# A four-layer graph network on one core: the recurrent part of n in seven block products, and the input part accumulated onto r times it

## The chip, the cores and the metric

The kernel runs on one core of a Trainium2 chip. The metric is the device time of one execution in microseconds. Three runs of the kernel before took 3054.23, 3055.60 and 3055.82 us; their median, 3055.6 us, is the time before. The engines are named as in the profile: PE is TensorE (PEld its weight loads), DVE is VectorE, ACT is ScalarE, POOL is GpSimd, SP is SyncE, which issues most of the DMAs.

## The reference

The input is 64 graphs of 256 nodes with 256 features, and one adjacency matrix (0 or 1) for each. Four layers follow one another, each of the form `x = x + layer(relu(layernorm(x)), adj)`. Layers 0, 1 and 2 are graph attention layers (four heads, four heads with a layer norm, one head). Layer 3 is a gated graph network: three rounds of aggregation over the adjacency and a GRU cell. The change touches the GRU cell alone:

```python
def _gru_cell(inp, h, w_ih, w_hh, b_ih, b_hh):
    gi = inp @ w_ih.T + b_ih
    gh = h @ w_hh.T + b_hh
    i_r, i_z, i_n = jnp.split(gi, 3, axis=-1)
    h_r, h_z, h_n = jnp.split(gh, 3, axis=-1)
    r = jax.nn.sigmoid(i_r + h_r)
    z = jax.nn.sigmoid(i_z + h_z)
    n = jnp.tanh(i_n + r * h_n)
    return (1.0 - z) * n + z * h
...
for i in range(L):
    m = jnp.einsum('bnd,de->bne', h, weight[i])
    aggr = jnp.einsum('bst,bsd->btd', A, m)
    h = _gru_cell(aggr, h, w_ih, w_hh, b_ih, b_hh)
```

Everything is fp32. `h_n` is called the recurrent part of n in what follows, and `i_n` its input part.

## The kernel before, in words

**Units.** `_fast_path` works through 33 units: one graph alone, then 31 pairs of graphs, then one graph alone (`units`). `graphs(u, first, nb)` lists the work of a unit of nb graphs: `layer0`, `layer1`, `layer2`, `gru`. A pair has S = 512 columns (nodes of graph 0, then of graph 1), N = 256 for each graph. Features lie on the 128 partitions in two chunks, `dc` for the features that are summed over and `j` for those that come out.

**Order of the work.** Nothing is issued while the work is listed. `op()` records each operation with its engine, an assumed cost, and the buffers it reads and writes, and `_Schedule` plans all of it at once. `paths()` gives first due times from the end of each unit (a multiple of `PACE`) back along the dependences, each step priced at `STRETCH` times the cost plus `MARGIN`. `play()` then goes forward in time: an idle engine takes the operation that is due first among those whose predecessors are done and whose buffers have a free slot. A result reaches another engine `HOP` ns after the operation ends. `latest()` plays the same work backwards for the next round's due times; after seven rounds at most the shortest plan is kept. The outcome is a fixed instruction order on each engine, so several units are in flight at once, and an engine that waits holds up all that is behind it. `HOP`, `STRETCH`, `MARGIN`, `PACE` and the costs given to `op()` take part in this plan alone; they issue nothing.

**Buffers.** The planner hands out fixed numbers of slots (lines 893 to 903), among them 13 of class `g` (128x512 fp32 partial results), 8 PSUM banks, 2 `ht3_` (the state h, transposed), 2 `ag` (the aggregated messages), 1 `am_r` (the adjacency), 3 `sw` (weight sums fetched from DRAM), 1 `turn`.

**The GRU of a pair, one round.** `aggregate` makes `ag` from `h` and the adjacency. The message weights have been multiplied into the input weights during setup (`wc`), so `ag` stands for the aggregated h. Then:

- `hidden(j, ...)`, for j = 0 and 1: `gate` multiplies `whh`'s block for n with the state `ht`, two matmuls of 512 columns into a bank of its own, and ScalarE moves the sum to SBUF with half the recurrent bias (`n`).
- `products` computes the sums for r and z. The four blocks (r or z, graph 0 or 1, state and message together) are arranged so that seven products of 256x256 by 256x256 serve where eight would: differences `t1` to `t4` on VectorE, seven calls of `product` (four matmuls of 256 columns each), and `kept` (ScalarE copies a bank to SBUF) or `added` (VectorE adds a bank to a buffer) after them. Three banks are used: `ps_s`, `ps_t`, `ps_w`.
- `unit(j, ...)`: ScalarE takes tanh of r (the sigmoids are written by tanh of half the argument); VectorE multiplies r with `n`; `gate` puts the input part into a new bank `ps_i`, two matmuls of 512 columns; VectorE adds it to `n` from PSUM; ScalarE takes tanh; z follows, and three VectorE operations make the new state, in place.
- `rows_of` transposes the new state for the next aggregation, or for the output.

Units of one graph go through `plain`, which the change leaves alone. In the profile, `gate`'s matmuls are L1477, `product`'s L1575, `aggregate`'s L1463, the differences in `products` L1567, and all that is recorded by `vec` is L912, whatever it is.

## Time and profile before

| what | value |
|---|---|
| median of three runs | 3055.6 us (3054.23 to 3055.82) |
| the profiled execution's own time | 3056.75 us |
| its span, first to last instruction | 3054.7 us |
| mean granted TensorE clock | 0.993 |
| busy: PE, PEld, DVE, ACT, POOL | 98%, 78%, 83%, 69%, 14% of the span |
| DMA | 212.43 MB, mean 70 GB/s |
| chain that ended last | PE 95% (L1575 37%, L1477 23%, L1267 12%, L1158 11%), DVE 2%, ACT 1%, DMA 1% |

All durations in the profile come from one profiled execution; its time is 1.15 us over the median of the runs, and its span 2.05 us under its own time. A line of a group reads: source line, engine, operation, output<-inputs, shapes, count, then busy time in us and mean ns of one, then the idle time of the engine ahead of these instructions and what ended it. A TensorE matmul of fp32 appears as two records, with a weight load ahead of each. Ends of matmuls are modelled, and their durations overlap; the time from one start to the next is the pace. A line of waits reads: who waited, for whom, us in total, how often, the longest.

### The profile page before, as it was taken

The page shows a single profiled execution, that of the slowest core. Times are in us where ns is not written, and L with a number is a line of the kernel's source. Part 1 is how long each engine was busy: PE and PEld are TensorE (multiplying, and loading weights), DVE is VectorE, ACT ScalarE, POOL GpSimd, SP SyncE. Part 2 cuts the span into 40 slices and gives each one's busy share as a digit, 9 for nine tenths or more (in the row PEclk, how much of TensorE's full clock was granted, in tenths as well). Part 3 has the DMA queues.
Part 4 walks back from the last instruction along what each step waited for, and adds up shares of the span by engine and source line. Part 5 has one row for each costly group of instructions (what it writes and reads, how often), then busy time and mean ns, then how long its engine had stood idle before and what let it go on. Part 6 is the DMA issues. An engine that isn't in the chain of part 4 may idle for free.

```text
span 3054.7 us, 56348 instructions
## 1 busy us (share of the span) xinstructions
PE 3000.5 (98%) x20900; PEld 2370.9 (78%) x20900; DVE 2533.0 (83%) x5933; ACT 2109.2 (69%) x4811; POOL 430.3 (14%) x643
## 2 busy tenths in 40 slices
PE   8799999999999999999999999999999999999998
PEld 7677787777787777787777787777777777787777
DVE  7876878888988888988888988888988888988764
ACT  7676667767776767766767766767776766766554
POOL 3311101111111111111111111111111111101100
PEclk9899999999999999999999999999999999999999
DMA  4111222221222122222121222221222221121110
GB/s 139 59 50 47 69 67 90 61 81 59 81 81 77 60 80 60 80 81 76 61 80 58 82 81 73 63 81 56 84 80 70 66 81 57 60 79 56 45 49 24
DMA packets 150936, 212.43 MB, mean 70 GB/s; under 512 B 49239, under 2 KB 102013, under 8 KB 143229
## 3 DMA queue, kind: packets, MB, share of 16 engines
q1 hardware_dynamic: 146752, 207.40, 21.7%
q8 instruction: 167, 2.74, 0.4%
q10 hardware_dynamic: 3900, 1.34, 0.2%
q14 instruction: 117, 0.95, 0.1%
HBM read 180.62 MB, written 19.68 MB: 66 GB/s over the span
## 4 chain that ended last, share of the span: by engine, by line
PE 95%; DVE 2%; ACT 1%; DMA 1%; issue 0%; POOL 0%; SPq 0%; ACTq 0%; DVEq 0%
PE bank L1575 37%; PE bank L1477 23%; PE bank L1267 12%; PE bank L1158 11%; PE bank L1463 6%; PE bank L1136 4%; PE bank L1491 3%; PE bank L1195 1%; DVE pt L912 1%; DVE g L912 0%; DVE o L912 0%; PE bank L1211 0%; PE bank L1032 0%; ACT g L912 0%; DMA xt<-in_x_dram 0%
## 5 line engine op out<-in xcount | busy, mean ns | idle before, releaser
L912 ACT ACTIVATE g<-g,bg 128x256 f32<-128x256 f32 (+1 forms) x756 | 393.9, 555 | 164.4 <-DVE g L912 96.6
L912 DVE SCALAR_TENSOR_TENSOR pt<-pt,f,cap 128x256 f32<-128x256 f32 x1152 | 476.2, 479 | 11.9 <-ACT pt L1248 10.1
L1248 ACT ACTIVATE pt<-cb,f 128x256 f32<-128x256 f32 x1062 | 441.3, 504 | 4.2 <-PE bank L1267 3.7
L1267 PEld LDWEIGHTS bank<-wh,pt 128*64 128x64 f32 (+1 forms) x8704 | 345.5, 141 | 85.5 <-issue 62.3
L1267 PE MATMUL bank<-wh,pt 128*64 128x65 f32 (+1 forms) x8704 | 391.3, 233 | 6.5 <-DVE pt L912 2.7
L912 DVE TENSOR_TENSOR g<-bank,g 128x512 f32<-128x512 f32 x279 | 191.4, 686 | 241.6 <-PE bank L1575 234.3
L1477 PE MATMUL bank<-ht,whh 128*128 128x512 f32 (+1 forms) x888 | 379.4, 561 | 0.0
L1477 PE MATMUL bank<-ag,wc 128*128 128x512 f32 (+1 forms) x888 | 377.9, 558 | 0.1
L1575 PE MATMUL bank<-g,sw 128*128 128x256 f32 x1488 | 349.8, 381 | 2.7 <-DVE g L1567 2.7
L912 DVE SCALAR_TENSOR_TENSOR g<-g,g 128x512 f32<-128x512 f32 (+1 forms) x396 | 257.2, 670 | 80.7 <-ACT g L912 80.5
L1575 PEld LDWEIGHTS bank<-g,sw 128*128 128x128 f32 x1488 | 278.7, 190 | 44.9 <-issue 4.5
L912 ACT ACTIVATE g<-bank,bg 128x256 f32<-128x256 f32 (+1 forms) x408 | 224.6, 568 | 108.3 <-PE bank L1477 97.6
L912 ACT COPY g<-bank 128x512 f32<-128x512 f32 x279 | 162.6, 583 | 187.8 <-PE bank L1575 181.9
L1477 PEld LDWEIGHTS bank<-ag,wc 128*128 128x128 f32 x888 | 164.4, 190 | 129.1 <-issue 120.1
L1477 PEld LDWEIGHTS bank<-ht,whh 128*128 128x128 f32 x888 | 161.1, 190 | 122.3 <-issue 103.6
L1463 PE MATMUL bank<-am_r,hl 128*128 128x256 f32 x1536 | 233.7, 301 | 0.0
L1119 ACT ACTIVATE xn<-xt,mv 128x256 f32<-128x256 f32 x384 | 210.5, 597 | 24.6 <-DVE mv L912 22.9
L1463 PEld LDWEIGHTS bank<-am_r,hl 128*128 128x128 f32 x1536 | 196.2, 189 | 31.8 <-issue 21.7
L1101 DVE BATCH_NORM_STATS2 st<-xt 128x6 f32<-128x256 f32 x512 | 207.9, 406 | 10.1 <-DMA xt<-in_x_dram 9.9
L912 ACT COPY ht<-bank 128x512 f32<-128x512 f32 (+1 forms) x264 | 143.4, 575 | 101.5 <-PE bank L1136 101.3
L1110 POOL TENSOR_SCALAR mv<-mv 128x4 f32<-128x4 f32 (+1 forms) x132 | 48.3, 366 | 1152.1 <-DVE mv L1102 1029.6
L1575 PE MATMUL bank<-ht,whh 128*128 128x256 f32 x744 | 180.2, 386 | 0.4 <-ACT ht L912 0.4
(113 smaller groups left out, 5389.9 us busy)
## 6 DMA issues: line engine op xcount, KB each, us to landing
sw<-sd SPq DMA_DIRECT2D x279, 256.0 KB, 2.7
cb<-rd SPq DMA_DIRECT2D x58, 1024.0 KB, 4.7
xt<-in_x_dram SPq DMA_DIRECT2D x31, 512.0 KB, 4.0
at<-in_adj_dram SPq DMA_DIRECT2D x31, 512.0 KB, 3.8
out_dram<-xt SPq DMA_DIRECT2D x31, 512.0 KB, 2.9
cb<-rd SPq DMA_DIRECT2D x29, 256.0 KB, 3.3
sd<-g SPq DMA_DIRECT2D x9, 256.0 KB, 2.3
cap<-cap_n SPq DMA_TRANSPOSE x128, 2.3
```

The source lines that it names most:

```text
L912: emit = lambda: fn(*[a() if callable(a) else a for a in args], **kw)
L1101: nc.vector.bn_stats(st.tile[:, c, :], xt.tile[:, c, :])
L1110: nc.gpsimd.tensor_scalar(mv.tile[:, 2, :], mv.tile[:, 1, :], 1e-5, None, op0=OP.add)
L1119: op("act", 610, lambda: nc.scalar.activation(xn.tile[:, c, :], xt.tile[:, c, :], AF.Relu, bias=mv.tile[:, 3, c : c + 1], scale=mv.tile[:, ...
L1136: nc.tensor.transpose(ps.tile[:, c * P : (c + 1) * P], xn.tile[:, c, dc * P : (dc + 1) * P], ident)
L1158: nc.tensor.matmul(ps.tile[:, : heads * W], lhsT=ht.tile[:, dc, c * P : (c + 1) * P], rhs=we[:, dc].rearrange("p h w -> p (h w)"), start=( ...
L1248: op("act", 500, lambda: nc.scalar.activation(pt.tile[:, b, jc, :], source(h, b), AF.Exp, scale=slope - 1.0, bias=f.tile[:, 1, h, c : c + ...
L1267: nc.tensor.matmul(ps[q * Q : (q + 1) * Q], lhsT=pt.tile[:, b, jc, i0 : i0 + Q], rhs=wh.tile[:, h, 2 * b + jc, :w], start=(jc == 0), stop= ...
L1463: nc.tensor.matmul(ps.tile[:, b * N : (b + 1) * N], lhsT=hl.tile[:, k, 2 * b + sc, :], rhs=am.tile[:, 2 * b + sc, :], start=(k == 0 and sc ...
L1477: nc.tensor.matmul(ps.tile[:, :S], lhsT=w[:, dc, g * P : (g + 1) * P], rhs=v.tile[:, dc, :], start=(first and dc == 0), stop=(last and dc ...
L1491: nc.tensor.transpose(ps.tile[:, c * P : (c + 1) * P], ht.tile[:, j, c * P : (c + 1) * P], ident)
L1575: nc.tensor.matmul(ps.tile[:, j * N : (j + 1) * N], lhsT=w()[:, dc, j * P : (j + 1) * P], rhs=view()[:, dc], start=(first and j == 0 and d ...
```

## The change

For pairs of graphs, `hidden` is rewritten. The four blocks of the recurrent part of n (output block j = 0 or 1, graph 0 or 1), each a sum over two chunks dc, are now computed with seven products of a 128x128 weight block by 128x256 columns in place of eight: four sums and differences of `whh`'s blocks for n are made once in setup (`sh`), three differences of state blocks for each round (`t23` with two parts, `t4`, beside `t1`, which is shared with `products`), and the products go to two banks, from which four ScalarE moves (`kept`) and three VectorE additions (`added`) build `ns`. A product that adds onto a half bank comes after the move that reads that half.

`unit` no longer takes a bank for the input part. VectorE writes (r+1) times `n` into a bank that `products` has finished with (`ps_w` for j = 0, `ps_t` for j = 1), the two `gate` matmuls accumulate the input part onto it, and ScalarE takes tanh straight from PSUM with the scale in the same instruction. The VectorE addition of the input part is gone. The recurrent part is now kept at scale 0.5 in all rounds, which needs a second copy of the bias (`bg` has ten columns).

The planner's constants change too: `PACE`, `HOP`, `STRETCH`, `MARGIN`, and the cost assumed for `aggregate`.

```diff
-PACE = 93600
+PACE = 93800
...
-    HOP = {"pe": 370, "act": 240, "dve": 240, "pool": 270, "sp": 0}
+    HOP = {"pe": 340, "act": 210, "dve": 210, "pool": 240, "sp": 0}
...
-    STRETCH = 3.79
-    MARGIN = 500
+    STRETCH = 3.43
+    MARGIN = 1100
...
+    block_of = lambda j, dc: whh[:, dc, 2 * D + j * P : 2 * D + (j + 1) * P]
+    less(lambda: sh[:, 0], lambda: block_of(1, 0), lambda: block_of(1, 1), [B_whh], [(B_sh, 0)], OP.add, 280)
+    less(lambda: sh[:, 1], lambda: sh[:, 0], lambda: block_of(0, 0), [B_whh, (B_sh, 0)], [(B_sh, 1)], cost=280)
+    less(lambda: sh[:, 2], lambda: block_of(0, 0), lambda: block_of(1, 0), [B_whh], [(B_sh, 2)], cost=280)
+    less(lambda: sh[:, 3], lambda: block_of(0, 1), lambda: sh[:, 1], [B_whh, (B_sh, 1)], [(B_sh, 3)], cost=280)
...
+        nc.vector.tensor_copy(bg[:, 8:10], bh.tile[:, 4:6])
...
-                op("pe", pe(1060), emit, [hl, am], [ps], takes=[ag])
+                op("pe", pe(1125), emit, [hl, am], [ps], takes=[ag])
...
-            def gate(ps, w, B_w, g, v, first, last):
+            def gate(ps, w, B_w, g, v, first, last, onto=False):
...
+                            skip_group_check=onto,
...
-                def hidden(j, ht, half):
-                    n, ps_h = g_tile(), bank()
-                    gate(ps_h, whh, B_whh, 4 + j, ht, True, True)
-                    vec(nc.scalar.activation, act(700), lambda: n.tile, lambda: ps_h.tile[:, :S], AF.Identity,
-                        bias=bg[:, 4 + j : 5 + j], scale=half, reads=[ps_h, B_bg], writes=[n], engine="act")
-                    return n
+                def hidden(ht, t1):
+
+                    ns = [g_tile() for _ in range(DC)]
+                    t23, t4 = buf("g", [P, 2, N]), buf("g", [P, N])
+                    ps_s, ps_w = bank(), bank()
+                    of = lambda g, dc: ht.tile[:, dc, g * N : (g + 1) * N]
+                    lo, hi = slice(0, N), slice(N, S)
+                    b0 = 4 if i == 0 else 8
+
+                    def less_of(out, x_, y_, reads, writes):
+                        op("dve", 415, lambda: nc.vector.tensor_tensor(out(), x_(), y_(), op=OP.subtract), reads, writes, port=True)
+
+                    def product(ps, where, w, v, reads, first=False):
+                        op("pe", 432, lambda: nc.tensor.matmul(
+                            ps.tile[:, where], lhsT=w, rhs=v(), start=first, stop=False, skip_group_check=True,
+                        ), [*reads, B_whh, B_sh], [ps])
+
+                    def kept(j, out, ps, where):
+                        vec(nc.scalar.activation, 440, lambda: ns[j].tile[:, out], lambda: ps.tile[:, where], AF.Identity,
+                            bias=bg[:, b0 + j : b0 + j + 1], scale=0.5, reads=[ps, B_bg],
+                            writes=[(ns[j], out.start)], engine="act")
+
+                    def added(j, out, ps, where):
+                        vec(nc.vector.scalar_tensor_tensor, 450, lambda: ns[j].tile[:, out], lambda: ps.tile[:, where], 0.5,
+                            lambda: ns[j].tile[:, out], op0=OP.mult, op1=OP.add, reads=[ps], writes=[(ns[j], out.start)])
+
+                    less_of(lambda: t23.tile[:, 1], lambda: of(1, 1), lambda: of(1, 0), [ht], [(t23, 1)])
+                    less_of(lambda: t23.tile[:, 0], lambda: of(1, 1), lambda: t1.tile[:, 0], [ht, t1], [(t23, 0)])
+                    less_of(lambda: t4.tile, lambda: of(0, 1), lambda: t23.tile[:, 0], [ht, (t23, 0)], [t4])
+                    product(ps_s, lo, block_of(0, 0), lambda: of(0, 0), [ht], True)
+                    product(ps_s, hi, block_of(0, 1), lambda: of(0, 1), [ht])
+                    kept(0, lo, ps_s, lo)
+                    added(0, lo, ps_s, hi)
+                    product(ps_w, lo, sh[:, 2], lambda: t23.tile[:, 1], [(t23, 1)], True)
+                    kept(1, hi, ps_w, lo)
+                    product(ps_s, lo, sh[:, 1], lambda: t23.tile[:, 0], [(t23, 0)])
+                    kept(1, lo, ps_s, lo)
+                    product(ps_s, lo, sh[:, 0], lambda: t1.tile[:, 0], [t1])
+                    added(1, hi, ps_s, lo)
+                    product(ps_w, lo, block_of(1, 1), lambda: t4.tile, [t4])
+                    added(1, lo, ps_w, lo)
+                    product(ps_s, lo, sh[:, 3], lambda: of(1, 1), [ht])
+                    kept(0, hi, ps_s, lo)
+                    return ns
...
-                    return (t2, t3), p1, ps_s
+                    return (t2, t3), p1, ps_s, (ps_w, ps_t)
...
-                    d, ps_i = g_tile(), bank()
+                    d, ps_n = g_tile(), free[j]
...
-                    vec(stt, dve(700), lambda: n.tile, lambda: d.tile, 1.0, lambda: n.tile,
-                        op0=OP.add, op1=OP.mult, reads=both, writes=[n], port=True)
-                    gate(ps_i, wi, B_wc, 4 + j, ag, True, True)
-                    vec(stt, dve(720), lambda: n.tile, lambda: ps_i.tile[:, :S], 2 * half, lambda: n.tile,
-                        op0=OP.mult, op1=OP.add, reads=[ps_i], writes=[n])
-                    vec(nc.scalar.activation, act(730), lambda: n.tile, lambda: n.tile, AF.Tanh,
-                        bias=bg[:, 6 + j : 7 + j], reads=[B_bg], writes=[n], engine="act")
+                    vec(stt, dve(700), lambda: ps_n.tile[:, :S], lambda: d.tile, 1.0, lambda: n.tile,
+                        op0=OP.add, op1=OP.mult, reads=[n, *both], writes=[ps_n], port=True)
+                    gate(ps_n, wi, B_wc, 4 + j, ag, False, True, True)
+                    vec(nc.scalar.activation, act(700), lambda: n.tile, lambda: ps_n.tile[:, :S], AF.Tanh,
+                        bias=bg[:, 6 + j : 7 + j], scale=2 * half, reads=[ps_n, B_bg], writes=[n], engine="act")
...
-                    ns = [hidden(j, ht, half) for j in range(DC)]
-                    rz = products(i, ht, ag, wi)
+                    t1 = buf("g", [P, DC, N])
+                    vec(nc.vector.tensor_tensor, 700, lambda t1=t1: t1.tile, lambda ht=ht: ht.tile[:, :, N:],
+                        lambda ht=ht: ht.tile[:, :, :N], op=OP.subtract, reads=[ht], writes=[t1], port=True)
+                    ns = hidden(ht, t1)
+                    rz = products(i, ht, t1, ag, wi)
```

## The prediction

> **What bounds the kernel now.** I read first the page's engine totals, then TensorE's waits, then the groups by shape, then the order in time, then the windows. The totals:
>
> ```profile
> span 3054.7 us, 56348 instructions
> PE 3000.5 (98%) x20900; PEld 2370.9 (78%) x20900; DVE 2533.0 (83%) x5933; ACT 2109.2 (69%) x4811; POOL 430.3 (14%) x643
> ```
>
> TensorE is 98% busy, but modelled matmul ends can hide gaps, so the view that decides is who TensorE waited for:
>
> ```profile
> PE bank L1136 <- ACT xn L1119: 29.0, 2, 14.8
> PE bank L1491 <- DVE ht L912: 3.9, 3, 1.9
> PE bank L1491 <- DVE hl L912: 2.8, 1, 2.8
> ```
>
> Two waits of 14.8 and 14.2 us, both before 105 us, are most of it. The same view cut to 400 to 2800 us is empty: there TensorE waits for nobody. So time is TensorE's instruction count times its pace. The pace comes from start-to-start times (columns: start, us, engine, line, op, count):
>
> ```profile
> 1570.61 3.60 PE L1477 MATMUL bank<-ag,wc 128*128 128x512 f32 x8
> 1574.04 1.89 PE L1575 MATMUL bank<-ag,wc 128*128 128x256 f32 x8
> 1575.77 0.60 PE L1136 MATMUL bank<-ident,xn 128*128 128x128 f32 x4
> ```
>
> Eight 512-column records take 1574.04-1570.61 = 3.43 us, 429 ns each; eight 256-column ones 1.73 us, 216 ns each. The mean durations (596 and 381 ns in the groups) are latencies that overlap and must not be summed. Each fp32 matmul is two records: 31 pairs of graphs x 3 GRU layers x 2 blocks j x 2 chunks dc = 372 matmuls is 744 records, as this group says:
>
> ```profile
> L1477 PE MATMUL bank<-ht,whh 128*128 128x512 f32 x744 | 344.5, 596 | 0.0
> L1575 PE MATMUL bank<-g,sw 128*128 128x256 f32 x1488 | 349.8, 381 | 2.7 <-DVE g L1567 2.7
> ```
>
> Who comes next? The steady pattern repeats every pair (chain pieces at 626.58, 718.39, 810.17 us: about 92 us). One period, and its two parts (columns: stretch, length, then busy us of PE, PEld, DVE, ACT, POOL):
>
> ```profile
> 1510.00:1581.00 71.00, 71.00 (x545) 54.00 (x544) 67.79 (x164) 49.87 (x111) 10.67 (x13) 1.00 0.21 63
> 1581.00:1592.00 11.00, 11.00 (x52) 9.63 (x51) 2.29 (x6) 7.19 (x16) 2.42 (x6) 1.00 0.12 30
> 1500.00:1592.00 92.00, 92.00 (x646) 72.44 (x645) 78.58 (x182) 65.97 (x150) 13.20 (x19) 1.00 0.23 73
> ```
>
> VectorE has 78.6 of 92 us, 85%, but unevenly: 95% for 71 us, then nearly idle for 11. It is the next limit.
>
> [...] a load takes 190 ns, yet 256-column records with a new load each start every 216 ns. [...]
>
> **The change part by part.** Per pair and GRU layer:
>
> *TensorE.* Removed: hidden()'s 4 matmuls of 512 columns, 8 x 429 = 3432 ns. Added: 7 of 256, 14 x 216 = 3024 ns. Saved 408 ns; x 93 = 37.9 us. The input gates keep their 4 matmuls; only their place moves. No other TensorE work changes.
>
> *Weight loads.* Six more records per layer: 6 x 190 ns x 93 = 106 us of load time, to some 2477 us (82%). Costed at nothing: each hides under a 216 ns matmul, with 26 ns to spare. Without that cover the price would be at most those 106 us.
>
> *VectorE.* The rows:
>
> ```profile
> L912 DVE SCALAR_TENSOR_TENSOR g<-bank,g 128x512 f32<-128x512 f32 x186 | 124.3, 684 | 14.0 <-PE bank L1477 13.8
> L912 DVE SCALAR_TENSOR_TENSOR g<-bank,g 128x256 f32<-128x256 f32 x12 | 5.1, 424 | 5.1 <-PE bank L1477 5.0
> L912 DVE TENSOR_TENSOR o<-o,beta_b 128x256 f32<-128x256 f32 x4 | 1.7, 422 | 0.1
> ```
>
> Removed: 2 additions of the input part (first row). Added: 3 differences (t23 twice, t4) and 3 additions out of PSUM (`added`), all of 256 columns. t1 is computed as before, only earlier. Back to back they cost less than their durations, since neighbours overlap:
>
> ```profile
> 2942.89 0.42 DVE L912 TENSOR_TENSOR o<-o,bias_b 128x256 f32<-128x256 f32 x1
> 2943.22 0.42 DVE L912 TENSOR_TENSOR o<-o,beta_b 128x256 f32<-128x256 f32 x1
> ```
>
> That is 0.34 us per step; 512-column ones step by 0.60. Net 6 x 0.34 - 2 x 0.60 = +0.84 us per layer, 2.5 us per period, 78 us in all; by full durations (6 x 423 - 2 x 684 ns) +1.17 us and 109 us. I take 78 and keep 109 as the upper end. That r times n is now written to PSUM has no row. [...] All this VectorE work lies beside TensorE's; it costs time only if TensorE runs dry.
>
> *ScalarE.* Two 512-column evictions become four of 256; the last tanh reads PSUM.
>
> ```profile
> L912 ACT ACTIVATE g<-bank,bg 128x512 f32<-128x512 f32 x186 | 124.6, 686 | 88.5 <-PE bank L1477 83.8 <-DVE rs L912 2.5
> L912 ACT ACTIVATE g<-bank,bg 128x256 f32<-128x256 f32 x222 | 100.0, 469 | 19.8 <-PE bank L1477 13.9 <-PE bank L1575 5.4 <-PE bank L1136 0.4
> L912 ACT ACTIVATE g<-g,bg 128x512 f32<-128x512 f32 x186 | 132.4, 716 | 12.6 <-DVE g L912 12.6
> ```
>
> 4 x 469 - 2 x 686 + 2 x (686 - 716) = +444 ns per layer, 41 us in all, at 72% of a period: hidden under TensorE.
>
> *New waits.* The seven products stand in a chain: TensorE, eviction, TensorE again on the same half bank. In each of two blocks the input gate waits for VectorE's product r times n. TensorE is in order, so behind a late one stand the matmuls of every graph in flight, attention of the next pair included, and ScalarE and VectorE then wait for those. The cover is other work: the old recurrence products have the same kind of chain (`kept`, `added`), and they cost no wait in the middle of the run. Exposed, one handoff is about 0.7 us of VectorE plus 0.15 (VectorE ends at 2983.35, the waiting transposes start at 2983.50). I take 2 us for the last pair, where cover thins, and bound the rest from 0 to 0.4 us per layer.
>
> *Setup and planner.* Four differences of 128x128 (281 ns by the nearest row) and a copy, about 1.3 us of VectorE before the first GRU matmul at 141 us; nothing. The planner's hop, stretch, margin and pace emit no instruction but re-order all. No DMA is added, and no queue gets another instruction. The edges (before 400 and after 2800 us) hold 48 us of TensorE waits; re-ordering may move them by some 10 us either way; I take zero.
>
> Sum: profiled execution 3056.75 us - 37.9 + 2 = 3020.9; the median of the runs is 1.15 below it, so 3019.7, say **3020 us**.
>
> **Rivals.**
>
> *Handoffs show* (0.15). TensorE stalls where the plan's cover is short: the hops assumed are 30 ns smaller than before, and thirteen buffers g hold more partial results at once. At 0.2 us per layer half the gain is gone: 3055.6 - 19 = 3037; at 0.41 all. Against: not one wait in 2400 us. For: nine dependent points per layer are new.
>
> *VectorE becomes the bound* (0.08), the one that ends slower. If VectorE can't exceed its present 85% of a period, its 2.5 us more need 2.5/0.855 = 2.9 us, x 31 = +91: 3147 us. It turns slower once the reachable share is below (78.6+2.5)/92 = 88%. For: idle VectorE time follows TensorE's results and can't simply be filled. Against: 95% is held for 71 us, and 8.7 us of idleness follow in the same period.
>
> *Edges shorten too* (0.05): the new order also cuts the first 105 us by 10: 3010.
>
> *Loads set the pace* (0.02): the change doesn't shorten TensorE, because seven separate matmuls, each with its own waits, lose their weight prefetch: 3055, no change.
>
> **How the numbers follow.** The likeliest case, whole gain with small losses, has 0.70 and its own range 3012 to 3030. From 3008 to 3045 I include it, the shorter edges and three quarters of the handoff case: about 0.85. Left out are the slower case, the no-change case and the worst handoffs. A measurement of this kernel can tell about 0.2% (6 us) from no change. Faster by more: 0.70 + 0.05 + 0.13 of the handoff case = 0.88; within: 0.02 + 0.02 = 0.04; slower: 0.08.
>
> **What would show it.** Right: no more 512-column ht,whh records in pairs (744 gone) and 1302 new 256-column ones at 216 ns pace; VectorE about 2610 us busy, ScalarE 2150, loads near 2477; TensorE's waits between 400 and 2800 us still under 5 us; a period near 90.7 us. Wrong: TensorE waits on DVE or ACT g or bank of tens of us in the middle (handoffs); VectorE over 95% with waits of TensorE for attention's pt (VectorE bound); pace above 216 ns in single products (loads).

## The result, and the profile after

The changed kernel takes **3045.64 us** (median of eight runs, 3044.02 to 3046.62); the kernel before, run beside it on the same chip, 3055.28 (3053.15 to 3055.82). The ratio is 0.9968, with a 95% interval of 0.9958 to 0.9978. So it is faster, by about 10 us. The forecast was 3020 with a range to 3045: the direction is right, the gain is a quarter of the one forecast, and the time lies 0.6 us outside the range.

The totals of the changed kernel, from the head of its page:

```profile
span 3044.8 us, 58325 instructions
...
PE 2974.3 (98%) x21458; PEld 2478.7 (81%) x21458; DVE 2606.7 (86%) x6310; ACT 2124.8 (70%) x4997; POOL 425.4 (14%) x643
```

TensorE has 558 records more, weight loads are 2478.7 us and VectorE 2606.7: all close to the forecast. The groups by shape show the new products (count after the x, then busy us and mean ns):

```profile
L1566 PE MATMUL bank<-g,sh 128*128 128x256 f32 x558 | 158.8, 383 | 0.4 <-DVE g L913 0.4
L1566 PE MATMUL bank<-ht,whh 128*128 128x256 f32 x372 | 101.5, 384 | 5.1 <-ACT ag L913 5.1
L1566 PE MATMUL bank<-ht,sh 128*128 128x256 f32 x186 | 55.8, 382 | 1.2 <-DVE g L913 1.2
L1566 PE MATMUL bank<-g,whh 128*128 128x256 f32 x186 | 55.5, 380 | 0.3 <-ACT g L913 0.3
...
L913 DVE SCALAR_TENSOR_TENSOR bank<-g,g 128x512 f32<-128x512 f32 x186 | 125.5, 691 | 4.5 <-ACT g L913 4.3
L913 ACT ACTIVATE g<-bank,bg 128x256 f32<-128x256 f32 x594 | 272.0, 471 | 164.1 <-PE bank L1623 100.1 <-PE bank L1566 47.5 <-PE bank L1486 11.7
```

558 + 372 + 186 + 186 = 1302 records, the number forecast, and TensorE waits 7 us for them in the whole run. Then who does TensorE wait for? First the whole run, then 600 to 2800 us (waiter, releaser: us in total, times, longest):

```profile
PE bank L1144 <- ACT xn L1127: 30.6, 2, 16.8
PE bank L1275 <- DVE pt L913: 6.7, 4, 3.8
PE bank L1501 <- DVE ht L913: 6.1, 5, 2.6
PE bank L1566 <- ACT ag L913: 5.1, 1, 5.1
```

```profile
PE bank L1623 <- DMA sw<-sd: 3.1, 6, 0.7
PE bank L1623 <- DVE g L913: 0.9, 1, 0.9
PE bank L1623 <- DVE pt L913: 0.5, 2, 0.3
```

From 600 to 2800 us TensorE waits 4.5 us. What has grown stands mostly ahead of that: `pt` of attention, 6.7 us in the whole run where before had

```profile
PE bank L1267 <- DVE pt L912: 2.7, 3, 1.8
```

and `ag` and `ht`. But the forecast had drawn its middle from 400 to 2800 us, where TensorE had waited for nobody before, and there the waits of the changed kernel add up to 9.2 us. The first of them:

```profile
PE bank L1623 <- DMA sw<-sd: 3.1, 6, 0.7
PE bank L1623 <- DVE g L913: 1.9, 2, 1.0
PE bank L1566 <- DVE g L913: 1.6, 2, 1.2
```

Now the windows. Before, then after (stretch, length, then busy us of PE, PEld, DVE, ACT, POOL, granted clock, DMA share, GB/s):

```profile
0.00:600.00 600.00, 556.79 (x4164) 449.39 (x4165) 478.77 (x1199) 409.11 (x980) 106.01 (x169) 0.97 0.24 73
600.00:2800.00 2200.00, 2199.93 (x15405) 1731.15 (x15404) 1882.27 (x4362) 1567.55 (x3551) 307.70 (x450) 1.00 0.23 72
```

```profile
0.00:600.00 600.00, 543.51 (x4278) 455.17 (x4278) 488.65 (x1264) 405.77 (x997) 108.97 (x170) 0.96 0.23 73
600.00:2800.00 2200.00, 2195.53 (x15937) 1830.56 (x15937) 1951.08 (x4684) 1590.90 (x3722) 301.36 (x451) 1.00 0.23 72
```

In the first 600 us TensorE is busy 13.3 us less than before, in the 2200 us after that 4.4 us less.

**An account that sees more.** Busy shares of 98% can't show 30 us, because the ends of matmuls are modelled. So I count every record at the pace that its kind keeps when nothing stops it, start to start (429 ns for 512 columns, 216 for 256, 217 for 257, 109 for the transposes, and so on), and call the rest of the span *gaps*. Gaps hold waits, but also matmuls at less than their pace.

| kernel | TensorE's work | gaps, 0 to 600 us | 600 to 2800 | after 2800 | span |
|---|---|---|---|---|---|
| before | 2943.6 | 68.7 | 26.6 | 15.7 | 3054.7 |
| after | 2905.7 | 91.5 | 34.7 | 13.0 | 3044.8 |

(The parts add up to the span within 0.1 us.) TensorE's work fell by 37.9 us. That figure is the forecast's own sum, 744 records at 429 ns against 1302 at 216; what the trace adds is that the counts are right, and that the new records start 216 ns apart in the median and 216.9 in the mean. The gaps grew by 28 us: 22.8 at the start, 8.1 in the middle, 2.7 less at the end. Cut at 400 us instead, where the forecast let its edge end, they grew by 11.7 us up to 400, by 19.0 from 400 to 2800, and shrank by 2.6 after that. Of the 22.8 us up to 600, 13.3 is idleness that the windows show; the other 9.5 us is TensorE running below its pace. One place where this can be seen, in the changed kernel's order in time (start, us from start to end, engine, line, operation, count, wait):

```profile
137.18 3.77 PE L1275 MATMUL bank<-wh,pt 128*128 128x257 f32 x8 [3.85 <-DVE pt L913]
140.74 1.91 PE L1144 MATMUL bank<-ident,xn 128*128 128x128 f32 x8
```

After a wait of 3.85 us, eight 257-column records take 140.74 - 137.18 = 3.56 us, 445 ns each; the same records take 217 ns in the middle of the run. So this wait cost its own length and, over these eight records, 8 x (445 - 217) ns = 1.8 us more.

So far this says where the time went. Why the new kernel has more gaps, the experiments ask. The candidates: the *order* that the planner made of the work; VectorE's *added work*; the *handoffs* of one half of the change or the other; the thirteen *buffers* `g`.

### The profile page after: what moved, and what is told of

Read it like the earlier page. It is cut to its first block, busy times and chain, and to the rows that moved or that the text cites. A ratio compares the mean times of both kernels' runs of the same rounds, so it can differ in the third digit from the quotient of the medians.

```text
span 3044.8 us, 58325 instructions
## 1 busy us (share of the span) xinstructions
PE 2974.3 (98%) x21458; PEld 2478.7 (81%) x21458; DVE 2606.7 (86%) x6310; ACT 2124.8 (70%) x4997; POOL 425.4 (14%) x643
## 4 chain that ended last, share of the span: by engine, by line
PE 90%; DVE 6%; ACT 1%; DMA 1%; POOL 1%; SPq 1%; issue 0%; ACTq 0%; DVEq 0%; POOLq 0%
PE bank L1623 34%; PE bank L1486 12%; PE bank L1166 11%; PE bank L1275 11%; PE bank L1566 9%; PE bank L1471 6%; PE bank L1144 4%; PE bank L1501 3%; DVE o L913 1%; DVE g L913 1%; DVE pt L913 1%; SPq L1352 1%; PE bank L1203 1%; DMA sw<-sd 1%; ACT pt L1256 1%; DVE mean L913 0%
## 5 line engine op out<-in xcount | busy, mean ns | idle before, releaser
L913 ACT ACTIVATE g<-bank,bg 128x256 f32<-128x256 f32 (+1 forms) x780 | 395.3, 522 | 222.0 <-PE bank L1623 100.1
L1256 ACT ACTIVATE pt<-cb,f 128x256 f32<-128x256 f32 x1062 | 465.0, 504 | 99.9 <-PE bank L1275 99.6
L913 DVE SCALAR_TENSOR_TENSOR pt<-pt,f,cap 128x256 f32<-128x256 f32 x1152 | 487.7, 477 | 18.1 <-ACT pt L1256 12.8
L913 ACT ACTIVATE g<-g,bg 128x256 f32<-128x256 f32 x570 | 267.1, 502 | 133.3 <-DVE g L913 105.2
L1486 PEld LDWEIGHTS bank<-ag,wc 128*128 128x128 f32 x888 | 160.6, 190 | 106.9 <-issue 95.4
L1471 PEld LDWEIGHTS bank<-am_r,hl 128*128 128x128 f32 x1536 | 202.4, 189 | 10.6 <-DVE hl L913 1.1
L1623 PE MATMUL bank<-ag,sw 128*128 128x256 f32 x744 | 179.1, 384 | 7.7 <-DVE g L913 4.1
L1623 PE MATMUL bank<-ag,wc 128*128 128x256 f32 x744 | 179.4, 384 | 0.7 <-ACT ag L913 0.7
L1623 PE MATMUL bank<-g,s 128*128 128x256 f32 x744 | 176.1, 380 | 0.0
L1623 PE MATMUL bank<-g,wc 128*128 128x256 f32 x744 | 175.9, 379 | 0.0
```

What stands on the lines that cost most here:

```text
L913: emit = lambda: fn(*[a() if callable(a) else a for a in args], **kw)
L1256: op("act", 500, lambda: nc.scalar.activation(pt.tile[:, b, jc, :], source(h, b), AF.Exp, scale=slope - 1.0, bias=f.tile[:, 1, h, c : c + ...
L1471: nc.tensor.matmul(ps.tile[:, b * N : (b + 1) * N], lhsT=hl.tile[:, k, 2 * b + sc, :], rhs=am.tile[:, 2 * b + sc, :], start=(k == 0 and sc ...
L1486: nc.tensor.matmul(ps.tile[:, :S], lhsT=w[:, dc, g * P : (g + 1) * P], rhs=v.tile[:, dc, :], start=(first and dc == 0), stop=(last and dc ...
L1623: nc.tensor.matmul(ps.tile[:, j * N : (j + 1) * N], lhsT=w()[:, dc, j * P : (j + 1) * P], rhs=view()[:, dc], start=(first and j == 0 and d ...
```

## The experiments

All ratios are to the kernel before on the same chip. "Constants" are those of the planner (`PACE`, `HOP`, `STRETCH`, `MARGIN`), which issue no instruction. Where a later experiment has constants of its own they were picked for a short plan in the planner's own reckoning; only their time on the chip counts here. That an order is the best for its kernel isn't claimed.

### Work and order apart: the constants exchanged

The changed kernel with the constants of before, and the reverse.

```diff
-PACE = 93800
+PACE = 93600
-    HOP = {"pe": 340, "act": 210, "dve": 210, "pool": 240, "sp": 0}
+    HOP = {"pe": 370, "act": 240, "dve": 240, "pool": 270, "sp": 0}
-    STRETCH = 3.43
-    MARGIN = 1100
+    STRETCH = 3.79
+    MARGIN = 500
-                op("pe", pe(1125), emit, [hl, am], [ps], takes=[ag])
+                op("pe", pe(1060), emit, [hl, am], [ps], takes=[ag])
```

> The changed kernel with the planner's constants of before (PACE, HOP, STRETCH, MARGIN, cost of aggregate). TensorE's work is the 37.9 us shorter one. Theory 1 (the new constants order the first 600 us badly, and cost the 23 us lost there): about 3022 us, TensorE's losses in the first 600 us back near 55 us. Theory 2 (the new dependences themselves leave TensorE without work while few graphs are in flight): 3040 us or more, with the losses of the first 600 us still 70 us or more.

> The kernel before with the planner's constants of after, and nothing else. Theory 1: the start gets worse here too, about 3075 us. Theory 2: within 6 us of the kernel before, about 3055 us.

Measured: the changed work in an order from the old constants **3297.85** (ratio 1.0792, 1.0774 to 1.0811); the old work in an order from the new ones **3075.18** (1.0065, 1.0048 to 1.0082). The first is far worse than either reading had it, and its start still has gaps of 94.7 us. The largest of its waits:

```profile
PE bank L1501 <- DVE ht L913: 107.7, 30, 6.8
```

Thirty times, once for nearly every pair, the transposes of the new state wait for VectorE, up to 6.8 us, and TensorE does nothing else in those 107.7 us. Same instructions, other order: 252 us, of which this one wait is 108. The second has the time of one reading and not its place: its start has gaps of 69.6 us, as before, and its loss lies in 600 to 2800 us (37.3) and after that (23.0). So the new constants alone do not make the slow start, and the old ones do not take it away.

### The two halves of the change, each alone

The seven products with the old `unit` (a bank of its own and the VectorE addition), and the new `unit` with the old `hidden`; both with the changed kernel's constants. Only the lines that matter are shown.

```diff
# products alone: in unit
-                    gate(ps_n, wi, B_wc, 4 + j, ag, False, True, True)
+                    gate(ps_i, wi, B_wc, 4 + j, ag, True, True)
+                    vec(stt, dve(720), lambda: n.tile, lambda: ps_i.tile[:, :S], 2 * half, lambda: n.tile, ...)
# accumulation alone: in gru
-                    ns = hidden(ht, t1)
+                    ns = [hidden(j, ht) for j in range(DC)]
```

> The changed kernel with only the seven block products; the input part goes to a bank of its own and is added by VectorE as before. TensorE's work is 37.9 us shorter than before, as in the whole change. If the wait of the input gate for r times n is what costs the start: about 3022 us. If the chain of seven products is what costs it: 3045 us or more, since VectorE has two additions more per round than in the whole change.

> The changed kernel with only the accumulation of the input part onto r times n; the recurrent part is four matmuls of 512 columns as before. TensorE's work is that of before. If the wait of the input gate is harmless: 3055 us or a little less, with VectorE's busy time about 112 us under that of before. If it costs the start: about 3078 us.

Measured: products alone **3351.19** (1.0969, 1.0951 to 1.0987), accumulation alone **3091.12** (1.0118, 1.0101 to 1.0135). Both are far on the slow side of what was expected. The first has the same kind of wait as above:

```profile
PE bank L1501 <- DVE ht L913: 85.1, 31, 12.8
```

The second does the same TensorE work as before with 92 us less of VectorE (2441.3), and is 36 us slower. That can't be read as the price of accumulating: the next experiments show what the order alone does. The two halves can't be priced by building one and letting the planner run.

### Work changed, order kept

Here the order of before stays, and only the size of some instructions changes: first TensorE's recurrent matmuls made 39.8 us shorter in sum by narrowing them, then VectorE's differences in `products` in part done twice.

```diff
# less TensorE work: in gate, for hidden only
-                            ps.tile[:, :S], lhsT=w[:, dc, g * P : (g + 1) * P], rhs=v.tile[:, dc, :],
+                            ps.tile[:, : S - narrow * dc * P], lhsT=w[:, dc, g * P : (g + 1) * P],
+                            rhs=v.tile[:, dc, : S - narrow * dc * P],
...
# more VectorE work: in less_of of products
+                            if out is t2:
+                                nc.vector.tensor_tensor(out.tile, x_(), y_(), op=OP.subtract)
+                            if out is t4:
+                                nc.vector.tensor_tensor(
+                                    out.tile[:, 0, :P], x_()[:, 0, :P], y_()[:, 0, :P], op=OP.subtract)
```

> The kernel before in its own order, with TensorE relieved by about what the change saves: in hidden, the second of the two matmuls of each block covers 384 of its 512 columns, so part of the recurrent part of n is left out. 4 records a round are 107 ns shorter, 428 ns x 93 = 39.8 us. If TensorE's work alone sets the time in a kept order: 3016 to 3022 us. If the other engines, at the pace that this order gives them, hold TensorE back as soon as it is faster: 3035 us or more, with new waits of TensorE in the middle of the run.

> The kernel before in its own order, with VectorE burdened by about what the change adds: in products, the difference t2 is computed twice, and 128 columns of t4 twice (0.60 + 0.2 us a round, about 75 us in all). If VectorE's work lies beside TensorE's, as the prediction has it: within 6 us of the kernel before. If VectorE is as much the bound as TensorE: tens of us slower, up to 3130 us.

Less TensorE work: **3015.48** (0.9871, 0.9855 to 0.9888), 40.2 us under its own neighbour of before (3055.67) for 39.8 us of work. Its gaps are those of before (66.9, 27.9, 14.7). So in this fixed order these 39.8 us of TensorE's work were worth their full length: the core of the forecast holds.

More VectorE work: **3094.18** (1.0133, 1.0116 to 1.0150). 87.6 us of VectorE cost 38.5 us. In the page's totals and in the waits of 600 to 2800 us:

```profile
PE 3009.7 (97%) x20900; PEld 2363.1 (76%) x20900; DVE 2620.6 (85%) x6119; ACT 2101.2 (68%) x4811; POOL 428.4 (14%) x643
```

```profile
PE bank L1158 <- DVE g L912: 19.2, 19, 1.0
```

VectorE is at 85% in sum, no more than in the changed kernel, yet TensorE now waits for it in nearly every period: 34 us of gaps were added in 600 to 2800. Since the order is kept, each of these waits can be found again in the trace of before. This one

```profile
1599.30 1.38 PE L1158 MATMUL bank<-w1e,ht 128*128 128x264 f32 x5 [1.00 <-DVE g L912]
```

is the matmul that started without a wait at 1580.10 us before, and so do the eighteen others fall 70 us into their period: at the end of the stretch of 71 us in which VectorE was already 95% busy. The waits are for `g` of L912 and not for the doubled differences themselves, which points to VectorE's queue as a whole coming late. "Hidden behind TensorE" was true of this kernel only as far as its order had room.

### Does VectorE's added work make the slow start?

The changed kernel in its own order, with the three additions out of PSUM (`added`) done for 32 of 256 columns; and the kernel before in its own order, with the addition of the input part done for 64 of 512.

```diff
# changed kernel, in added
+                        out, where = (slice(c.start, c.start + 32) for c in (out, where))
# kernel before, in unit
-                    vec(stt, dve(720), lambda: n.tile, lambda: ps_i.tile[:, :S], 2 * half, lambda: n.tile,
+                    vec(stt, dve(720), lambda: n.tile[:, :64], lambda: ps_i.tile[:, :64], 2 * half, lambda: n.tile[:, :64],
```

> The changed kernel in its own order, with VectorE relieved of most of what the change adds: the three additions `added` in hidden cover 32 of their 256 columns, so most of two blocks of the recurrent part of n is left incomplete. Every wait and every instruction stays; VectorE's work falls by about 3 x 0.23 us a round, 64 us. If VectorE's added work is what took the missing 28 us: 3025 us or less. If it is the new waits and the order, whatever VectorE has to do: 3040 us or more.

> The kernel before in its own order, with VectorE relieved: the addition of the input part covers 64 of 512 columns, so most of the input part of n is left out. VectorE's work falls by about 80 us. If before was bound by TensorE alone: 3050 us or more, since TensorE waited for almost nothing. If VectorE was already holding it: 3045 us or less.

Measured: the changed kernel with 55 us less of VectorE **3044.61** (0.9954, 0.9940 to 0.9968), 1 us better by the times and some 4 by the ratios, whose intervals meet; the kernel before with 78 us less **3054.73** (0.9996, 0.9989 to 1.0003), no difference. Waits of the changed kernel with light additions, beside those shown above:

```profile
PE bank L1144 <- ACT xn L1127: 30.6, 2, 16.5
PE bank L1275 <- DVE pt L913: 6.5, 3, 4.1
PE bank L1566 <- ACT ag L913: 5.1, 1, 5.1
```

They are the same waits. So in an order that was planned with VectorE's work in it, the amount of that work isn't what took the 28 us. The rival "VectorE becomes the bound" falls for these orders. That the planner made a worse order because it had more VectorE work to place isn't touched by this.

### The same work in other orders

The changed kernel with other constants (`PACE` 94200, `STRETCH` 3.64, `MARGIN` 950, `HOP` 355/225/225/255); the kernel before with others (`PACE` 94200, `STRETCH` 3.81); and the accumulation alone with others (`PACE` 93300, `STRETCH` 3.5, `MARGIN` 200, `HOP` 340/210/210/240).

> The changed kernel with other planner constants (PACE 94200, STRETCH 3.64, MARGIN 950, HOP 355, 225, 225, 255), no other edit: another order of the same instructions. If the missing 28 us are a matter of the order, this one, with fewer gaps on TensorE in its plan, takes about 3030 us. If they belong to the change's dependences in any order: 3042 us or more.

> The kernel before with PACE 94200 and STRETCH 3.81, no other edit. If the order alone is worth as much as the change's measured gain: about 3040 us, below the changed kernel. If the order before was as good as orders get: 3053 us or more.

> Only the accumulation of the input part onto r times the recurrent part (as e4_onto_only), with an order of its own: PACE 93300, STRETCH 3.5, MARGIN 200, HOP 340. TensorE's work is that of before, VectorE's some 94 us under it. If VectorE is a limit beside TensorE: about 3035 us, below the whole change although TensorE saves nothing. If only TensorE's work counts: 3050 us or more.

| work | orders measured, us |
|---|---|
| before | 3055.3, 3075.2, **3043.7** |
| accumulation alone | 3091.1, **3043.2** |
| the whole change | 3045.6, 3297.9, **3037.3** |

Intervals of the three new ones: 0.9938 (0.9921 to 0.9955) for the change, 0.9962 (0.9948 to 0.9976) for before, 0.9956 (0.9940 to 0.9973) for the accumulation. The re-ordered change and the accumulation each fell between their two readings; the kernel before came out near its first. Two things follow. First, the kernel before, merely put in another order, is as fast as the changed kernel: the order is worth as much as the gain measured. Second, accumulation alone and the kernel before end equal (3043.2 and 3043.7) with equal TensorE work and 86 us of VectorE between them: the page of the accumulation says

```profile
PE 2997.1 (99%) x20900; PEld 2370.1 (78%) x20900; DVE 2448.0 (80%) x5752; ACT 2108.1 (69%) x4811; POOL 449.3 (15%) x643
```

against 2534.1 for the kernel before in its other order. The lighter VectorE alone bought nothing here, in one good order of each.

The re-ordered kernel before has fewer gaps in the first 600 us (57 for 68.7). The re-ordered changed kernel has 79.8 there: less than 91.5, still more than any order of before.

### Which rounds make the slow start?

A graph's GRU runs three rounds. The seven products can be used in some of them only, with the old four wide matmuls in the others:

```diff
-                    ns = hidden(ht, t1)
+                    ns = hidden(ht, t1) if i < 2 else [whole(j, ht) for j in range(DC)]
```

(`whole` is the old `hidden` at scale 0.5; the input part is accumulated in all rounds.) First rounds 0 and 1; then the last round alone; the last round alone with 15 buffers `g` for 13; the middle round alone. All have constants of their own.

> The whole change, but the seven block products only in the first two of the three GRU rounds, four matmuls of 512 columns in the last; PACE 92900, STRETCH 3.54, MARGIN 250. TensorE saves two thirds of 37.9 us, 25.3; VectorE's work is some 20 us under that of before instead of 74 over it. If the two engines have to be balanced: about 3010 us, faster than both kernels. If TensorE's work alone counts: 3030 us at best, a third of the change's saving behind the best order of the whole change (3037 us) minus nothing.

> The block products in the last of the three GRU rounds alone, whole matmuls in the first two, the accumulation in all; PACE 93800, STRETCH 3.93, MARGIN 700, HOP 340. TensorE saves 12.6 us. If the last round is where the blocks disturb the order: 3070 us or more, slower than before. If any round is like another: about 3030 us, as for the middle round.

> As e13_last_round, with 15 buffers of class g in place of 13, no other edit. If the last round's blocks suffer because two pairs' rounds are in flight at once and share the buffers of partial results: some 30 us faster than e13_last_round, about 3045 us. If buffers don't matter: within 10 us of e13_last_round.

> The block products in the middle round alone; PACE 92400, STRETCH 3.81, MARGIN 0, HOP 355. TensorE saves 12.6 us, as in e13_last_round. If the last round is what disturbs: about 3025 us. If any round is like another: no better than e13_last_round by more than 10 us.

| products in | time, us | ratio (95%) | TensorE's work | VectorE busy | gaps: 0 to 600, 600 to 2800, rest |
|---|---|---|---|---|---|
| rounds 0, 1 | 3015.82 | 0.9867 (0.9851 to 0.9884) | 2918.4 | 2580.8 | 49.8, 33.5, 14.1 |
| last round | 3048.07 | 0.9974 (0.9964 to 0.9984) | 2931.0 | 2491.4 | 61.0, 38.7, 15.5 |
| last round, 15 `g` | 3035.68 | 0.9933 (0.9917 to 0.9950) | 2931.0 | 2501.4 | 66.1, 25.0, 13.0 |
| middle round | 3024.11 | 0.9895 (0.9878 to 0.9911) | 2931.0 | 2523.4 | 52.2, 27.9, 13.5 |

Leaving the products out of the last round costs TensorE 12.7 us more work than the whole change, and the kernel is 29.8 us faster than the changed one, 21.5 faster than the changed one's best order. VectorE's work is then 48 us *above* that of before, not below as I had expected. It is 26 us under the changed kernel's, but there 55 us less had bought almost nothing, so a relieved VectorE isn't the reason. The last round alone missed both of its readings (3070 or more, about 3030); the middle round alone took the time expected of it if the last is what disturbs. At equal TensorE work, the last round alone is 24 us behind the middle round alone. Windows of the last round alone, then of the middle round alone:

```profile
0.00:600.00 600.00, 563.73 (x4442) 460.87 (x4443) 489.01 (x1254) 420.36 (x1019) 113.37 (x170) 0.98 0.25 76
600.00:2800.00 2200.00, 2193.75 (x15444) 1755.84 (x15442) 1851.56 (x4362) 1557.23 (x3588) 381.93 (x453) 1.00 0.22 72
```

```profile
0.00:600.00 600.00, 570.40 (x4329) 468.14 (x4330) 491.79 (x1247) 418.44 (x1009) 108.11 (x171) 0.98 0.26 77
600.00:2800.00 2200.00, 2200.00 (x15596) 1761.54 (x15596) 1887.71 (x4379) 1568.61 (x3619) 299.67 (x450) 1.00 0.24 72
```

The middle round keeps TensorE busy for all of 2200 us, with more VectorE work; the last round loses 6.3 us there and 6.7 at the start. Two more buffers `g` gave the last round 12.4 us back, in the middle of the run and not at the start. That is a little more than the 10 us allowed for buffers that don't matter and less than half of the 30 expected if they are the cause, and the order is another one too.

### Is it the round or one order's luck? Do more buffers help the whole change?

Other constants for rounds 0 and 1 (`PACE` 94700, `STRETCH` 3.96, `MARGIN` 0, `HOP` 370/240/240/270), others for the last round alone (`PACE` 94700, `STRETCH` 3.25, `MARGIN` 1200, `HOP` 370/240/240/270), and the whole change with `"g": (slots, 15)` (`PACE` 92200, `STRETCH` 3.96, `MARGIN` 900, `HOP` 355/225/225/255).

> As e11_two_rounds (blocks in the first two rounds), in another order: PACE 94700, STRETCH 3.96, MARGIN 0, HOP 370. If the gain of e11_two_rounds comes from leaving the last round alone: within 10 us of its 3015.8 us. If it was a lucky order: 3035 us or more.

> As e13_last_round (blocks in the last GRU round alone, 13 buffers g), in another order: PACE 94700, STRETCH 3.25, MARGIN 1200, HOP 370. If the last round's blocks disturb any order: 3035 us or more, at least 10 us behind the middle round's 3024.1 us. If e13_last_round was an unlucky order: about 3025 us.

> The whole change, blocks in all three rounds, with 15 buffers of class g in place of 13 and PACE 92200, STRETCH 3.96, MARGIN 900, HOP 355. If the shared buffers of partial results are the larger part of what the last round costs: 3020 us or less. If they are a smaller part: between 3022 and 3037 us. If none: 3037 us or more, as e7_new_order.

| kernel | time, us | ratio (95%) | gaps: 0 to 600, 600 to 2800, rest |
|---|---|---|---|
| rounds 0, 1, second order | **3011.86** | 0.9857 (0.9841 to 0.9874) | 50.8, 26.4, 14.4 |
| last round, second order | 3044.17 | 0.9963 (0.9949 to 0.9977) | 68.8, 30.5, 11.9 |
| all rounds, 15 `g` | 3041.92 | 0.9956 (0.9939 to 0.9973) | 75.5, 39.5, 17.8 |

The last round stays 20 us behind the middle one in a second order, and rounds 0 and 1 stay far ahead of all three rounds in a second order. Fifteen buffers brought nothing to the whole change beyond what other constants did (3037.3 with thirteen). Over all twenty kernels the gaps of the first 600 us divide: 75 to 95 us in the six that have the products in all rounds, 50 to 73 us in the fourteen others. The six stand for only five orders and the fourteen for eleven, and the two groups nearly touch (75.5 and 73.0). Cut at 400 us, the same count shows more:

| kernel | gaps, 0 to 400 us | 400 to 2800 | after 2800 |
|---|---|---|---|
| before | 66.6 | 28.8 | 15.8 |
| before, constants of after | 66.7 | 40.1 | 23.1 |
| before, its third order | 53.7 | 31.6 | 15.3 |
| the whole change | 78.3 | 47.8 | 13.2 |
| the whole change, other constants | 68.5 | 48.0 | 16.0 |
| the whole change, 15 `g` | 66.7 | 48.5 | 17.8 |
| rounds 0, 1 | 46.9 | 36.4 | 14.3 |
| rounds 0, 1, second order | 48.0 | 29.3 | 14.6 |
| middle round | 49.6 | 30.5 | 13.8 |
| last round | 56.8 | 42.9 | 15.7 |
| last round, second order | 66.5 | 32.8 | 12.0 |

Up to 400 us two of these three orders of the whole change lose about what before lost, so most of the 11.7 us there belongs to one order and not to the change. From 400 to 2800 us all three have 19 to 20 us more than before; the order from the old constants, not in the table, has far more. The divide of the first 600 us lies in its last third: from 400 to 600 us the six have 8.8 to 21.4 us of gaps, the others 2.1 to 8.0. And the gain of rounds 0 and 1 has two parts: 11 to 19 us fewer gaps than the whole change from 400 to 2800 us, and some 20 fewer up to 400 than its two better orders, of which the kernel before found 13 as well, by order alone.

Rounds 0 and 1 in the second order beat both kernels: 44 us under before, 34 under the changed kernel. Its totals and windows:

```profile
span 3010.1 us, 57586 instructions
...
PE 2966.9 (99%) x21272; PEld 2434.0 (81%) x21272; DVE 2568.9 (85%) x6124; ACT 2127.1 (71%) x4935; POOL 411.3 (14%) x643
```

```profile
0.00:600.00 600.00, 568.42 (x4432) 474.82 (x4433) 507.42 (x1293) 425.02 (x1028) 103.21 (x171) 0.99 0.26 77
600.00:2800.00 2200.00, 2200.00 (x15787) 1798.41 (x15787) 1928.49 (x4536) 1597.14 (x3683) 296.76 (x455) 1.00 0.23 72
```

TensorE has 25.2 us less work than before, the gaps are 19.4 us less, and TensorE is busy for all of the middle: the two add up to 44.6, the difference of the spans. About 11 us of the 19 is what the kernel before gained too when it was put in another order.

## Why the prediction was right or wrong

**TensorE's pace and work: right.** The counts came as forecast, and the 1302 new records start 216 ns apart in the median and 216.9 in the mean. That such work is worth its length was shown with the order kept (40.2 us for 39.8). The busy shares of before (98% for TensorE's matmuls with their modelled ends, 78% for its weight loads, 83% for VectorE) did not by themselves show TensorE to be the bound. The narrowed matmuls do, with the lightened VectorE that changed nothing (3054.73 us, ratio 0.9996).

**Weight loads: right.** 2478.7 us for 2477. The rival "loads set the pace" falls: after 1244 of the 1302 new records the next one starts within 217 ns, with a load of 190 ns between.

**VectorE's work: size right, "costed at nothing" only in part.** Busy time rose by 73.7 us for 78. In an order that was planned for it, 55 us of it cost 1 to 4 us. In an order that wasn't, 87.6 us cost 38.5. The cover that I named (TensorE's work beside it) had to be arranged for, and the end of the 71-us stretch at 95% that I had shown myself was the place where it broke.

**The write to PSUM: right.** I took nothing for it, with no row of before to go by. The group of r times n takes 691 ns, where the same operation into SBUF was among rows of 686 before: 5 ns more, 0.9 us over the 186.

**ScalarE: too high, with no effect.** Busy time rose by 15.6 us, not 41. The durations in sum did rise by 39.9, but neighbours overlap; I had added up durations after having corrected VectorE for just that.

**New waits and their cover: the larger part of the step that failed.** I bounded the new waits by 0 to 0.4 us per pair and layer and took nothing of that, only 2 us for the last pair, because TensorE had not waited once from 400 to 2800 us. In just that stretch the gaps grew by 19.0 us, 0.20 us per pair and layer, and by 19.2 and 19.7 in two other orders of the whole change. That TensorE waited for nobody before didn't mean that an order of the new work would have as much cover. Of the 19.0 us, 9.2 are waits that the profile shows, over the limit of 5 that I had set: 4.6 for `g` of VectorE and ScalarE, 3.1 for weight sums that arrive by DMA. The rest is TensorE starting records later than its pace; what holds it up isn't known. The period, between the casts of the adjacency sixteen pairs apart, is 91.0 us (852.0 to 2308.0) for 91.8 before (829.5 to 2298.2): 0.8 us saved for the 1.2 of TensorE's work.

**Setup and planner: the other part.** I put "some 10 us either way; I take zero" on the edges. They measured +11.7 us up to 400 us and -2.6 after 2800, +9.1 together, and +2.1 in each of two other orders. With the 19.0 us that makes 28 us where the sum had 2, and 28 of the 37.9 us are gone. The error wasn't only one of size: I priced an order by its edges, as though the planner would make an equally good one from other work. With the very same instructions the orders measured here differ by 4 to 260 us, so the uncertainty of that term was as large as the gain, and the range should have said so.

**The rivals.** The time is nearest to "handoffs show" (3037, 0.15), which took 0.2 us per layer in the middle of the run: that size and that stretch fit. Its sign, tens of us of waits on `g` or on a bank, did not come: 4.6 us. So the profile shows its mechanism for a quarter of the 19.0 us. "VectorE becomes the bound" is not what happened, and "edges shorten" had the wrong sign.

**What stays open.** Why the whole change has 19 to 20 us more gaps from 400 to 2800 us in three orders. The products of the last round have a large part in it, since without them 11 to 19 us go; but the kernel before in the order of the new constants also has 40.1 us there, so an order alone can cost as much, and two orders of a kernel can't exclude that one work was given better orders than another. The middle round alone was measured in one order only. More of `g` helps the last round alone and not the whole change, in orders that differ as well, so the share of the buffers isn't known. What the accumulation is worth by itself in a good order is bounded only by 3043.2 against 3043.7: nothing found.

## What to carry to other kernels

Take a saving on the busiest engine at its full length only while the order of the work stays (here 40.2 us for 39.8); when a planner makes the order anew, price the new order as a term of its own, with a range from measured re-orderings of unchanged work. Before crediting or blaming a change, run the kernel before in another order as well: here that alone gave 12 us, more than the change did. And where a change can be made in some of several like stages, try the subsets: the one that did less of it was faster by 34 us.

## What was not expected of the hardware

After one of its waits TensorE was slow for a while. Right after this wait of 3.85 us, eight records of 257 columns started 445 ns apart in the mean, where the middle of the run has 217, and the transposes behind them 213 ns apart for 109. The windows of the changed kernel show the granted clock (the 0.50 and the 1.00):

```profile
136.25:143.07 6.82, 5.89 (x17) 4.76 (x18) 6.62 (x16) 4.63 (x9) 4.44 (x7) 0.50 0.57 174
143.07:146.00 2.93, 2.93 (x14) 2.31 (x13) 1.84 (x4) 2.93 (x7) 0.82 (x2) 1.00 0.03 5
```

TensorE resumed at 137.18 us and stayed at half the clock until 143.07, for 5.89 us. The paces agree with the 0.50: 445/217 is 2.05. So by an estimate this one wait of 3.85 us cost about another 5.89 / 2 = 2.9 us.

The granted clock between 100 and 200 us was 0.94 before and 0.90 after, with 95.4 and 88.6 us of TensorE busy:

```profile
100.00:200.00 100.00, 95.36 (x680) 77.26 (x681) 79.74 (x225) 75.35 (x182) 23.52 (x37) 0.94 0.23 70
```

```profile
100.00:200.00 100.00, 88.60 (x656) 74.74 (x657) 83.64 (x235) 73.69 (x178) 24.71 (x36) 0.90 0.19 59
```

In the clock records of the first 600 us TensorE is busy at half the clock for 18.5 us before and 30.1 us after. Records at that clock took 445 ns for 217, about half of the time lost, so the difference, 11.6 us, stands for an estimated 5.8 of the 9.5 us of slower pace in the account above. The changed kernel with the old constants, which waits far more (a mean granted clock of 0.973 for 0.991), is busy at half the clock for 136 us in its whole run, the changed kernel itself for 30: by the same estimate half of the difference, some 53 of the 252 us that it is slower, came on top of the waits.
